# Two tiles' values and one tile's scores moved into the last chunk of the first layer of a two-layer fp32 kernel

## The chip, the core and the metric

The kernel runs on one core of a Trainium2 chip, in one launch, all of it in 32-bit floats. The core has five instruction queues that run side by side and wait for each other through semaphores: PE (TensorE, with its weight loads shown as PEld), DVE (VectorE), ACT (ScalarE), POOL (GpSimd) and SP (SyncE, which here only issues DMAs). The metric is the device time of one execution in microseconds (us), lower is better. Three runs of the kernel before took 5859.45, 5865.35 and 5869.25 us; the median is 5865.35 us.

## The reference, cut to what matters

The input `x` has 4 images of 384 channels by 64 by 64 pixels. Each of two layers normalises its input over groups of channels (`_gn`) and adds its result to that input.

```python
x = x + _L0_conv_ref(_gn(x), ...)   # a selective state-space layer over the 4096 pixels of an image
x = x + _L1_conv_ref(_gn(x), ...)   # an outlook-attention layer
```

The first layer projects each pixel to 768 channels and their gates, runs a causal convolution of 4 taps, derives a step size, `B` and `C` from it, and runs the recurrence `h = dA * h + dBx` over the 4096 pixels with 16 states a channel; the output is gated and projected back to 384 channels.

The second layer works on 3 by 3 windows at stride 2, 32 by 32 windows an image. For each window it needs scores and values:

```python
a = einsum('bchw,ac->bhwa', pooled, attn_w) + attn_b      # pooled: 2x2 means; 12 heads x 9 x 9 scores
a = softmax(a.reshape(B, L, HEADS, 9, 9) * scale)          # over the last axis
v = einsum('blkc,koc->blko', patches, conv_w)              # 9 pixels q of a window, a 384x384 matrix for each
o = einsum('bnlpq,bnlqd->bnlpd', a, v)                     # attention inside the window
out[..., ki::2, kj::2] += o                                # the windows are folded back with their overlaps
y = einsum('bchw,oc->bhwo', out, proj_w) + proj_b
```

## The kernel before, in words

**First layer** (`mamba_layer`). The 4 images are cut into 68 chunks of 241 pixels, 17 an image. The work of a chunk is 12 units of 64 channels, so 816 units; the main loop counts them as steps `s`, and chunk 67, the last, is steps 804 to 815. In step `s` the loop issues, for every engine, the parts of several units: DVE runs the two scans of unit `s` (`s_scan`, 128x968 each) and half of the products that feed unit `s+1` (`s_inputs2`); ACT makes the decays of unit `s+1` (`s_decay`, 8 exponentials into the two PSUM tiles `da0`, `da1`); POOL multiplies the states of unit `s-1` by `C` (`s_outputs`, 128x1928) and makes the other half of the products of unit `s+2` (`s_inputs`); PE sums the states of two units (`s_sum`) in every odd step. SP fetches `dxr` for units `s+4, s+5` and `dtr` for units `s+2, s+3` in every even step (`s_fetch`, `s_fetch_dt`). Each engine runs its instructions strictly in the order in which the Python code issues them: the helper `InOrder` fixes that, so an instruction that waits holds up all that its engine has behind it. Tile, the framework, puts in the semaphore waits. Its DMAs take eight semaphores in turn, whichever engine issues them: a DMA waits until the one eight places before it has landed.

The parts for the chunk to come (`plan`) end with the last chunk. `e_project`, `e_mean` and `e_store` (`ends`) project a finished chunk back, add up its statistics and store it to `x1` in DRAM; for chunk 67 they stand in steps 818 to 823, followed by the group norm of the last image (`group_norm_coeffs`: matmul `pm`, two ACT operations, matmuls `pv`, one DVE and one POOL operation, and the factors `sc1`, `bi1`, `bi4`).

**Second layer** (`outlook_layer`). An image is cut into 8 tiles of 8 pixel rows, 128 windows each, so 32 tiles. For each tile: three loads of its rows `xr`, pooled pixels `t2`, scores (six matmuls `psa<-wa,t2` of 128x486), a softmax (`at`, `mx`, `rs` on DVE, ACT and POOL), a store of the weights to DRAM (`ads`) and reads back as `ain` in another layout, block diagonals `bd` (ACT and POOL), 36 small matmuls `ps<-bd,vin` for each of four window rows (`p_attend`), six DVE adds into `fold` (`p_fold`), and the output projection (`pso`). The values of a tile are 9 products `psv<-wv,xp` (three matmuls of 128x384 each), copied by ACT and stored to DRAM, from where they come back as `vin`.

Tiles 0 to 21 have their values computed during the first layer, on pixels that are already normalised (class `Early`, functions `v_load` to `v_next`, up to chunk 65); they are marked by `c.vd`, and layer 2 only reads them. Their pooled pixels come from POOL (`pool_rows`) and the last product of the softmax is POOL's. Tiles 22 to 31 have no `vd`: their pixels are put in order by six ACT operations (`pixels`), and the nine products of tile `i+1` run on PE while tile `i` is attended (`p_values`). Tile 31 of the loop ends the kernel.

**Between the layers** (`outlook_before`). This is a generator that the main loop resumes once a step, at the end of the step, from `front_end`, step 803, on: the front of layer 1 is over then and its SBUF (right side) is free.

```python
        if s >= front_end:
            over = das[0] if s >= NU * len(chunks) - 1 else None
            behind(lambda: pmm.tile([P, 2, TM], F32, tag="mm", name="psv").rearrange("p a b -> p (a b)"), over)
```

Before the change it loads the rows of tile 0, writes zeros to the ends of some DRAM buffers, loads the value matrices `wv` (9 parts of 576 KB) in the steps 803 to 807, two a step, has POOL pool tile 0, loads `wa`, `ab`, `wpr`, `pb` and `own`, waits for step 815, and then has PE compute the scores of tile 0 into `da0`, which is free after the last scan. Four steps later it issues their softmax.

Of the kernel before, what the change touches and what calls it, by code (L numbers as in the profile page):

```python
# [7 lines left out]
F32 = mybir.dt.float32  # L8
AF = mybir.ActivationFunctionType
# [3 lines left out]
P = 128  # L13
C = 384
# [96 lines left out]
def mamba_layer(ctx, tc, x, w, x1, sc1, bi1, bi4, consts, early, behind):  # L111
# [837 lines left out]
    for s in range(-4, NU * (len(chunks) + 2)):  # L949
        k, m = divmod(s, NU)  # L950
        if m % 2 == 0 and unit(s + 4) is not None:
            s_fetch(s + 4)
        if m % 2 == 0 and unit(s + 2) is not None:
            s_fetch_dt(s + 2)
        parts(s, EARLY)
        if m % 4 == 3 or s >= NU * len(chunks):
            norm_part(False)

        if (u := unit(s + 1)) is not None:
            s_inputs2(u)  # L960
        if (u := unit(s - 3)) is not None and not u.first and u.j % 2:
            s_gate(u)
        parts(s, READY)

        b, ci = chunks[k][:2] if 0 <= k < len(chunks) else (B, 0)
        if b + 1 < B:
            n, e = divmod(NU * ci + m - 3, NU // 2)
            if e == 0 and 0 < n <= NCB * NX:
                x_stat(b + 1, n - 1, pending.pop())
            if e == 1 and 0 <= n < NCB * NX:  # L970
                pending.append(x_load(b + 1, n))
            if e == 2 and n == NCB * NX:
# [24 lines left out]
        if s >= front_end:  # L997
            over = das[0] if s >= NU * len(chunks) - 1 else None
            behind(lambda: pmm.tile([P, 2, TM], F32, tag="mm", name="psv").rearrange("p a b -> p (a b)"), over)


class OutlookTile:
# [146 lines left out]
def outlook_layer(ctx, tc, x1, w, out, sc1, bi1, bi4, weights, ready, tiles):  # L1149
# [23 lines left out]
        InOrder(tc, e) for e in (nc.tensor, nc.vector, nc.scalar, nc.gpsimd, nc.sync)  # L1173
    )

    wa, ab, wv, wpr, pb, own, vds, ads = (
        weights[name] for name in ("wa", "ab", "wv", "wpr", "pb", "own", "vds", "ads")
    )
    io = ctx.enter_context(tc.tile_pool(name="io1", bufs=3))
    act = ctx.enter_context(tc.tile_pool(name="act1", bufs=2))  # L1180
    pa = ctx.enter_context(tc.tile_pool(name="pa", bufs=1, space=bass.MemoryType.PSUM))
    pv = ctx.enter_context(tc.tile_pool(name="pv", bufs=3, space=bass.MemoryType.PSUM))
    pt = ctx.enter_context(tc.tile_pool(name="pt", bufs=1, space=bass.MemoryType.PSUM))

    def p_load(c):
        if c.vd is not None and c.i % 3 == 0 and tiles[c.i + 3].vd is not None:
            xr = act.tile([P, 3, NCB, ROWS, NW], F32, tag="xp", name="xr")
            xr = xr.rearrange("p k cb r w -> p (k cb r w)")[:, : NCB * ROWS * W]
            c.load(sp, x1, xr.rearrange("p (cb r w) -> p cb r w", cb=NCB, w=W))
            return  # L1190
        c.load(sp, x1, io.tile([P, NCB, ROWS, W], F32, tag="xr", name="xr", bufs=4))

    def p_pixels(c):
        t2 = act.tile([P, NCB, NR * NW], F32, tag="t2", name="t2")
        if c.vd is not None:
            t3 = act.tile([P, VQ, C], F32, tag="vst", name="t3", bufs=3).rearrange("p q c -> p (q c)")
            t3 = t3[:, : NCB * NR * W].rearrange("p (cb i j) -> p cb i j", cb=NCB, j=W)
            c.pool_rows(gp, ae, t2, t3, sc1, bi4)
            return
        t3 = act.tile([P, NCB, NR * NW], F32, tag="t3", name="t3", bufs=1)  # L1200
        xp = act.tile([P, 3, NCB, ROWS, NW], F32, tag="xp", name="xp")
        for _ in c.pixels(gp, ae, xp, sc1, bi1):
            pass
        c.pool(ve, t2, t3)
# [20 lines left out]
            )  # L1225

    def fetch(c, r, name, width, src):
        dst = act.tile([GW * KK, NGW, width], F32, tag=name, name=name, bufs=3)
        n = GW * KK
        row = r * NW * KK  # L1230
        full = min(NGW, (src.shape[0] - row) // n)
        sp.dma_start(dst[:, :full, :], src[row : row + full * n, :].rearrange("(g p) a -> p g a", p=n))
        if full < NGW:
            sp.dma_start(dst[: src.shape[0] - row - full * n, full, :], src[row + full * n :, :])
        return dst
# [7 lines left out]
    def p_blocks(c, r, part, parts):  # L1243

        n = GW * KK
        if part == 0:
            c.bd[r] = act.tile([n, NGW, GW, HO], F32, tag="bd", name="bd")
        bd = c.bd[r]
        mine = 1 + r % 2
        if part == 0:  # L1250
# [23 lines left out]
                    )  # L1274

    def p_clear(c):
        c.fold = fold = act.tile([P, NCB, ROWS, W + 2], F32, tag="fold", name="fold")
        if c.first:
            gp.memset(fold, 0.0)
        else:  # L1280
            gp.memset(fold[:, :, 1:, :], 0.0)
            gp.tensor_copy(fold[:, :, 0, :], tiles[c.i - 1].fold[:, :, ROWS - 1, :])
# [74 lines left out]
    for i in range(-1, len(tiles)):  # L1357
        mid, old = tile_at(i + 1), tile_at(i)
        even = mid is not None and (mid in ready or mid.vd is not None)
        for r in range(NR):  # L1360
            t = NR * i + r
            if i < 0 and r == 3:
                p_fetch_values(mid, 0)
            if old and r == 0 and i > 0:
                p_fetch_values(old, 0)
# [18 lines left out]
            if t == 1:  # L1384
                for c in ready:
                    p_load(c)
            c, k = ahead(old, mid, r + 1)
            qs = ((0, 1, 2), (3, 4), (5, 6), (7, 8))[r]
            for n, q in enumerate(qs):
# [31 lines left out]
                    stores.pop(0)()  # L1421


def outlook_before(ctx, tc, w, x1, H, W, sc1, bi4, dram, weights, ready, tiles):

    nc = tc.nc
    pe, ve, ae, gp, sp = (
        InOrder(tc, e) for e in (nc.tensor, nc.vector, nc.scalar, nc.gpsimd, nc.sync)  # L1430
    )
    NW = W // 2
    HO = HEADS * KK
    wp = ctx.enter_context(tc.tile_pool(name="wv1", bufs=1, side="right"))
    wv = weights["wv"] = wp.tile([P, NCB, KK, C], F32, tag="wv", name="wv")
    t2 = wp.tile([P, NCB, NR * NW], F32, tag="t2", name="t2")
    c = tiles[0]
    ready.append(c)
    with tc.tile_pool(name="before", bufs=1, side="right") as early:
        c.load(sp, x1, early.tile([P, NCB, ROWS, W], F32, tag="xr", name="xr"))  # L1440

        zero = early.tile([KK, C], F32, tag="zero", name="zero")
        gp.memset(zero, 0.0)
        vds = weights["vds"] = [dram.tile([P * KK + KK, C], F32, tag=f"vd{i}", name=f"vd{i}") for i in range(2)]
        ads = weights["ads"] = [dram.tile([P * KK + KK, HO], F32, tag=f"ad{i}", name=f"ad{i}") for i in range(3)]
        for v in vds:
            sp.dma_start(v[P * KK :, :], zero)
        for v in ads:
            sp.dma_start(v[P * KK :, :], zero[:, :HO])
        for q in range(KK):  # L1450
            sp.dma_start(wv[:, :, q, :], w["wv"][:, :, q, :])
            if q % 2:
                psum, over = yield
        c.pool_rows(gp, ae, t2, early.tile([P, NCB, NR, W], F32, tag="t3", name="t3"), sc1, bi4)
        yield
    wp = ctx.enter_context(tc.tile_pool(name="wp1", bufs=1, side="right"))
    na = HO * KK
    shapes = {
        "wa": [P, NCB, na],
        "ab": [P, na],  # L1460
        "wpr": [P, NCB, NCB, P],
        "pb": [P, NCB],
        "own": [GW * KK, GW],
    }
    for name, shape in shapes.items():
        weights[name] = wp.tile(shape, F32, tag=name, name=name)
    for cb in range(NCB):
        sp.dma_start(weights["wa"][:, cb], w["wa"][:, cb])
    for name in ("ab", "wpr", "pb", "own"):
        sp.dma_start(weights[name], w[name])  # L1470
    while True:
        psum, over = yield
        if over is not None:
            break
    parts = c.weights(
        pe, ve, ae, sp, over.rearrange("p (h a) -> p h a", h=2), wp, weights["wa"], weights["ab"], ads[0]
    )
    next(parts)

    for _ in range(4):  # L1480
        yield
    next(parts)
    next(parts, None)


@with_exitstack
def layers(ctx, tc, w, out):
# [24 lines left out]
    later = outlook_before(ctx, tc, w, x1, H, W, sc1, bi4, dram, weights, ready, tiles)  # L1512

    def behind(*room):
        try:
# [76 lines left out]
```

## Time and profile before

| what | us |
|---|---|
| median of three runs | 5865.35 |
| the profiled execution, its own time | 5861.92 |
| its span, first to last instruction | 5860.1 |
| PE, DVE, ACT, POOL busy | 5295.0, 5241.6, 4848.9, 5392.2 |
| first layer: last POOL product of the states ends at | 4955.4 |
| second layer: first attention matmul at | 4982.4 |

Every number below is in microseconds from the start of the span. In the views of the timeline a line is: start, duration, engine, source line (53 is the helper that records all operations), operation, output<-inputs, shapes, how many were merged, and in brackets the idle time of that engine before it with what ended it. The trace shows each 32-bit matmul of the program as two rows, so 27 matmuls of the program are 54 in it. "SPq" are DMA issues on SP. The line "PEclk" or the column of that name is the clock that TensorE was granted, as a part of full speed.

### The profile page before, as it was taken

Reading aid. Unit: us, or ns where it says so; the run is one execution under the profiler, and the core shown is the slowest. Engines: PE = TensorE matmul, PEld = TensorE weight load, DVE = VectorE, ACT = ScalarE, POOL = GpSimd, SP = SyncE. Lnnn points to the kernel's source line nnn. Section 1 sums busy time; section 2 is a strip of 40 time slices with the busy share of each in tenths; the row PEclk is TensorE's granted clock in tenths of the full one; section 3 lists DMA queues with packets and bytes.
Section 4 is the critical chain, followed back from the end, with each engine's and each line's share of the span. In section 5 each row is a group of like instructions: output and inputs, shape, how many; then the busy total and the mean of one; then the engine's idle time right before and its main releaser. Section 6 shows DMA issues by size and latency. Waiting matters only on the chain.

```text
span 5860.1 us, 126156 instructions
## 1 busy us (share of the span) xinstructions
PE 5295.0 (90%) x46114; PEld 3820.7 (65%) x46114; DVE 5241.6 (89%) x4269; ACT 4848.9 (83%) x13283; POOL 5392.2 (92%) x2045
## 2 busy tenths in 40 slices
PE   6888888888999999998999999999999995899999
PEld 5666666666666666666666666666666663666555
DVE  4999999999999999999999999999999997787444
ACT  4888888888888888888898888889889885677665
POOL 3999999999999999999999999999999998899433
PEclk9999999999999999999999999999999997999999
DMA  4555554445666666666666666656666655666444
GB/s 133 145 142 143 143 144 134 131 131 139 166 169 174 171 179 162 173 171 159 176 177 174 179 168 171 170 148 173 170 167 169 162 152 158 199 211 206 159 168 154
DMA packets 758875, 955.11 MB, mean 163 GB/s; under 512 B 211488, under 2 KB 660972, under 8 KB 758124
## 3 DMA queue, kind: packets, MB, share of 16 engines
q1 hardware_dynamic: 758252, 947.04, 58.7%
q8 instruction: 362, 5.93, 0.4%
q14 instruction: 261, 2.14, 0.1%
HBM read 720.92 MB, written 225.70 MB: 162 GB/s over the span
## 4 chain that ended last, share of the span: by engine, by line
ACT 36%; PE 25%; DVE 17%; DMA 5%; POOL 5%; SPq 4%; issue 4%; DVEq 0%; ACTq 0%; POOLq 0%
ACT da L53 20%; DVE h L53 14%; PE ps_in L53 4%; SPq L53 4%; POOL h L53 4%; PE ps_v L53 4%; PE y L53 3%; PE psv L53 3%; ACT L53 3%; PE ps_cv L53 2%; PE ps L53 2%; ACT zs L53 2%; PE pso L53 2%; ACT xc L53 2%; PE psa L53 2%
## 5 line engine op out<-in xcount | busy, mean ns | idle before, releaser
L53 DVE TENSOR_TENSOR_SCAN h<-da,h 128x968 f32<-128x968 f32 x1632 | 3453.9, 2158 | 151.6 <-POOL h L53 74.7
L53 POOL TENSOR_TENSOR h<-h,bc 128x1928 f32<-128x1928 f32 x816 | 3231.1, 3960 | 45.2 <-DVE h L53 41.3
L53 ACT ACTIVATE da<-dtr,alog 128x241 f32<-128x241 f32 x6528 | 2657.5, 455 | 370.0 <-DVE h L53 291.1
L53 POOL TENSOR_TENSOR h<-dxr,bc 128x964 f32<-128x964 f32 x816 | 1622.8, 1989 | 65.7 <-DMA dxr<-dxd 48.7
L53 PE MATMUL ps_in<-u,win 128*128 128x241 f32 x4824 | 1056.9, 370 | 37.2 <-ACT xb L53 26.4
L53 PEld LDWEIGHTS ps_in<-u,win 128*128 128x128 f32 x4824 | 903.7, 190 | 161.2 <-ACT xb L53 49.1
L53 DVE TENSOR_TENSOR h<-dxr,bp 128x964 f32<-128x964 f32 x816 | 928.7, 1138 | 10.5 <-DMA dxr<-dxd 9.2
L53 PE MATMUL y<-h,ssum 128*32 128x241 f32 x13056 | 782.9, 373 | 70.9 <-POOL h L53 70.7
L53 PE MATMUL ps_cv<-xb,cdiag 128*128 128x241 f32 x3264 | 718.1, 373 | 26.6 <-ACT zs L53 21.3
L53 PEld LDWEIGHTS ps_cv<-xb,cdiag 128*128 128x128 f32 x3264 | 606.3, 190 | 133.7 <-issue 34.0
L53 PEld LDWEIGHTS y<-h,ssum 128*32 128x32 f32 x13056 | 434.6, 111 | 343.6 <-POOL h L53 93.3
L53 POOL TENSOR_TENSOR bd<-ain,own 99x1188 f32<-99x1188 f32 x192 | 431.0, 2266 | 211.4 <-PE ps L53 196.9
L53 PE MATMUL ps_out<-zs,wout 128*128 128x241 f32 (+1 forms) x2448 | 563.8, 382 | 0.0
L53 ACT ACTIVATE bd<-ain,own 99x216 f32<-99x216 f32 (+1 forms) x1408 | 467.5, 420 | 113.1 <-PE ps L53 102.2
L53 PEld LDWEIGHTS ps_out<-zs,wout 128*128 128x128 f32 x2448 | 489.2, 200 | 43.2
L53 PE MATMUL ps_v<-wq,xo 128*32 128x384 f32 x4752 | 425.0, 489 | 32.4 <-ACT xr L53 29.8
L53 DVE TENSOR_TENSOR fold<-fold,ps 128x192 f32<-128x192 f32 (+1 forms) x768 | 210.3, 302 | 185.2 <-PE ps L53 171.8
L53 PE MATMUL ps_dt<-xd,wdt 128*128 128x241 f32 x816 | 227.1, 403 | 91.4 <-ACT xd L53 52.9
L53 PEld LDWEIGHTS ps_v<-wq,xo 128*32 128x32 f32 x4752 | 140.8, 110 | 240.5 <-issue 163.3
L53 PE MATMUL pso<-fold,wpr 128*128 128x256 f32 (+6 forms) x990 | 275.4, 425 | 3.7 <-DVE fold L53 3.3
L53 PE MATMUL ps<-bd,vin 99*32 99x99 f32 (+1 forms) x9216 | 228.2, 250 | 46.4 <-DVE fold L53 21.1
L53 PEld LDWEIGHTS ps<-bd,vin 99*32 99x32 f32 (+1 forms) x9216 | 200.5, 109 | 102.8 <-issue 44.8
(128 smaller groups left out, 5544.8 us busy)
## 6 DMA issues: line engine op xcount, KB each, us to landing
dxr<-dxd SPq DMA_DIRECT2D x1632, 120.5 KB
dtr<-dtd SPq DMA_DIRECT2D x1632, 120.5 KB
wq<-in_wv SPq DMA_DIRECT2D x297, 192.0 KB
dxd<-dtx SPq DMA_DIRECT2D x816, 60.2 KB
dtd<-dt SPq DMA_DIRECT2D x272, 180.8 KB
ve<-v SPq DMA_DIRECT2D x198, 192.0 KB
bc<-bcd SPq DMA_DIRECT2D x272, 120.5 KB
vin<-ve SPq DMA_DIRECT2D x66, 445.5 KB
```

Source lines behind the costliest of these rows:

```text
L53: made = self.tc.keep_in_program_order(issue(*args, **kwargs))
```

## The change

The generator is rewritten, `outlook_layer` gets its buffers from other pools, and tiles 22 and 23 get a `vd`.

1. Nothing but allocations stands in step 803. In step 804 come the zeros, the rows of tile 0 and a third of `wa`, in step 805 the rest of `wa`; `wv` is loaded by ninths, part `q` in step 805+q; `ab` and `own` in step 814. `wpr` and `pb` are loaded by layer 2 itself, in its second step of tile 0.
2. POOL pools tile 0 in step 806. The scores of tile 0 are computed in three parts of 128x324 in steps 807 to 809, each copied from PSUM by ACT (`ae.mul`); the softmax is issued in step 815, not 819.
3. Tile 22: rows loaded in step 807, put in order in step 808 (`put`), its nine values computed in steps 809 to 815: one a step, two in steps 812 and 814. Each is copied by ACT, which also issues its store (`ae.dma_start`).
4. Tile 23: rows loaded in step 815, put in order in step 816, its nine values in step 825, one after the other. On PE they come between the matmul `pm` and the matmuls `pv` of the last group norm.
5. `outlook_layer`: `ain`, `vin`, `bd`, `fold` come from a pool `hot`, `xp` and `t3` from `far`, `wpr` and `pb` from `wp1`; the numbers of buffers are unchanged. The first `vin` is fetched as the first DMA of the layer, not behind the first `ain` and `xr`. In the loop over tiles only tiles 24 to 31 compute their values.

```diff
-            over = das[0] if s >= NU * len(chunks) - 1 else None
-            behind(lambda: pmm.tile([P, 2, TM], F32, tag="mm", name="psv").rearrange("p a b -> p (a b)"), over)
+            behind(lambda: pmm.tile([P, 2, TM], F32, tag="mm", name="psv"), s >= NU * len(chunks) - 1)
...
+    hot = ctx.enter_context(tc.tile_pool(name="hot1", bufs=2))
+    far = ctx.enter_context(tc.tile_pool(name="far1", bufs=2))
+    wp = ctx.enter_context(tc.tile_pool(name="wp1", bufs=1))
+    wpr = wp.tile([P, NCB, NCB, P], F32, tag="wpr", name="wpr")
+    pb = wp.tile([P, NCB], F32, tag="pb", name="pb")
...
-        if c.vd is not None and c.i % 3 == 0 and tiles[c.i + 3].vd is not None:
-            xr = act.tile([P, 3, NCB, ROWS, NW], F32, tag="xp", name="xr")
+        if c.vd is not None and c.i % 3 == 0 and tiles[c.i + 2].vd is not None:
+            xr = far.tile([P, 3, NCB, ROWS, NW], F32, tag="xp", name="xr")
...
-            if i < 0 and r == 3:
+            if i < 0 and r == 0:
                 p_fetch_values(mid, 0)
...
                 for c in ready:
                     p_load(c)
+                sp.dma_start(wpr, w["wpr"])
+                sp.dma_start(pb, w["pb"])
...
+        def values(i, q):
+            v = staged()
+            psv = room().rearrange("p a b -> p (a b)")[:, :C]
+            last[i].values(pe, wv, q, psv)
+            ae.copy(v, psv)
+            ae.dma_start(last[i].vd.rearrange("(p q) c -> p q c", q=KK)[:, q, :], v)
+
+        def scores(h):
+            psa = room().rearrange("p a b -> p (a b)")[:, :NH]
+            for cb in range(NCB):
+                pe.matmul(
+                    psa, t2[:, cb, :], wa[:, cb, h * NH : (h + 1) * NH], start=(cb == 0), stop=(cb == NCB - 1)
+                )
+            ae.mul(at[:, h * NH : (h + 1) * NH], psa, 0.25)
...
+            for q in {1: (0,), 2: (1,), 3: (2,), 4: (3,), 5: (4,), 6: (5,), 7: (6,), 8: (7,), 9: (8,)}.get(n, ()):
+                load_wv(q)
+            if 3 <= n < 6:
+                scores(n - 3)
+            if n == 3:
+                last[0].load(sp, x1, rows())
...
+        GROUP = {4: (("put", 0),), 5: ((0, 0),), 6: ((0, 1),), 7: ((0, 2),), 8: ((0, 3), (0, 4)), 9: ((0, 5),), 10: ((0, 6), (0, 7)), 11: ((0, 8), ("load", 1)), 12: (("put", 1),), 13: (), 14: (), 15: (), 16: (), 21: ((1, 0), (1, 1), (1, 2), (1, 3),(1, 4), (1, 5), (1, 6),(1, 7), (1, 8)), 22: ()}
+
+        for n in range(max(GROUP) + 1):
+            room, over = yield
+            first(n)
+            for item in GROUP.get(n, ()):
+                if item[0] == "put":
+                    put(item[1])
+                elif item[0] == "load":
+                    last[item[1]].load(sp, x1, rows())
+                else:
+                    values(*item)
+            if over and not done:
+                done.append(n)
+                softmax()
...
+    last = tiles[len(early.tiles) : 3 * NT]
+    for i, c in enumerate(last):
+        c.vd = dram.tile([P * KK, C], F32, tag=f"vl{i}", name=f"vl{i}")
```

The `n` of the diff is the step less 804.

More of the change, by code (lines that the diff above doesn't have):

```diff
@@ L1174, in outlook_layer @@
     )
-    wa, ab, wv, wpr, pb, own, vds, ads = (
-        weights[name] for name in ("wa", "ab", "wv", "wpr", "pb", "own", "vds", "ads")
-    )
+    wa, ab, wv, own, vds, ads = (weights[name] for name in ("wa", "ab", "wv", "own", "vds", "ads"))
     io = ctx.enter_context(tc.tile_pool(name="io1", bufs=3))
     act = ctx.enter_context(tc.tile_pool(name="act1", bufs=2))
+    hot = ctx.enter_context(tc.tile_pool(name="hot1", bufs=2))
[3 more added lines that the diff above has]
+    pb = wp.tile([P, NCB], F32, tag="pb", name="pb")
     pa = ctx.enter_context(tc.tile_pool(name="pa", bufs=1, space=bass.MemoryType.PSUM))
@@ L1199, in p_pixels @@
             return
-        t3 = act.tile([P, NCB, NR * NW], F32, tag="t3", name="t3", bufs=1)
-        xp = act.tile([P, 3, NCB, ROWS, NW], F32, tag="xp", name="xp")
+        t3 = far.tile([P, NCB, NR * NW], F32, tag="t3", name="t3", bufs=1)
+        xp = far.tile([P, 3, NCB, ROWS, NW], F32, tag="xp", name="xp")
         for _ in c.pixels(gp, ae, xp, sc1, bi1):
@@ L1227, in fetch @@
     def fetch(c, r, name, width, src):
-        dst = act.tile([GW * KK, NGW, width], F32, tag=name, name=name, bufs=3)
+        dst = hot.tile([GW * KK, NGW, width], F32, tag=name, name=name, bufs=3)
         n = GW * KK
@@ L1246, in p_blocks @@
         if part == 0:
-            c.bd[r] = act.tile([n, NGW, GW, HO], F32, tag="bd", name="bd")
+            c.bd[r] = hot.tile([n, NGW, GW, HO], F32, tag="bd", name="bd")
         bd = c.bd[r]
@@ L1276, in p_clear @@
     def p_clear(c):
-        c.fold = fold = act.tile([P, NCB, ROWS, W + 2], F32, tag="fold", name="fold")
+        c.fold = fold = hot.tile([P, NCB, ROWS, W + 2], F32, tag="fold", name="fold")
         if c.first:
@@ L1421, in outlook_layer, with outlook_before @@
                     stores.pop(0)()
-def outlook_before(ctx, tc, w, x1, H, W, sc1, bi4, dram, weights, ready, tiles):
+def outlook_before(ctx, tc, w, x1, H, W, sc1, bi1, bi4, dram, weights, ready, tiles, last):
     nc = tc.nc
@@ L1433, in outlook_before @@
     HO = HEADS * KK
+    na = HO * KK
+    NH = na // 3
     wp = ctx.enter_context(tc.tile_pool(name="wv1", bufs=1, side="right"))
-    wv = weights["wv"] = wp.tile([P, NCB, KK, C], F32, tag="wv", name="wv")
-    t2 = wp.tile([P, NCB, NR * NW], F32, tag="t2", name="t2")
+    shapes = {"wv": [P, NCB, KK, C], "wa": [P, NCB, na], "ab": [P, na], "own": [GW * KK, GW]}
+    for name, shape in shapes.items():
+        weights[name] = wp.tile(shape, F32, tag=name, name=name)
+    wv, wa, ab = (weights[name] for name in ("wv", "wa", "ab"))
@@ L1437, in outlook_before @@
     c = tiles[0]
     ready.append(c)
+    vds = weights["vds"] = [dram.tile([P * KK + KK, C], F32, tag=f"vd{i}", name=f"vd{i}") for i in range(2)]
+    ads = weights["ads"] = [dram.tile([P * KK + KK, HO], F32, tag=f"ad{i}", name=f"ad{i}") for i in range(3)]
     with tc.tile_pool(name="before", bufs=1, side="right") as early:
-        c.load(sp, x1, early.tile([P, NCB, ROWS, W], F32, tag="xr", name="xr"))
-        zero = early.tile([KK, C], F32, tag="zero", name="zero")
-        gp.memset(zero, 0.0)
@@ L1444, in outlook_before @@
[L1444 to L1450, printed above, removed]
-            sp.dma_start(wv[:, :, q, :], w["wv"][:, :, q, :])
-            if q % 2:
-                psum, over = yield
@@ L1454, in outlook_before @@
[L1454 to L1483, printed above, removed]
+        pixels = lambda: early.tile([P, 3, NCB, ROWS, NW], F32, tag="xp", name="xp")
@@ new lines, in outlook_before, with load_wv @@
+        rows = lambda: early.tile([P, NCB, ROWS, W], F32, tag="xr", name="xr")
+        staged = lambda: early.tile([P, C], F32, tag="v", name="v1", bufs=3)
+        at = early.tile([P, na], F32, tag="at", name="at")
+        mx = early.tile([P, HO], F32, tag="mx", name="mx")
+        rs = early.tile([P, HO], F32, tag="rs", name="rs1")
+        t2 = early.tile([P, NCB, NR * NW], F32, tag="t2", name="t2")
+        def load_wv(q):
+            sp.dma_start(wv[:, :, q, :], w["wv"][:, :, q, :])
+        def values(i, q):
[4 more added lines that the diff above has]
+            ae.dma_start(last[i].vd.rearrange("(p q) c -> p q c", q=KK)[:, q, :], v)
@@ new lines, in scores, with put, first @@
+        def scores(h):
[5 more added lines that the diff above has]
+            ae.mul(at[:, h * NH : (h + 1) * NH], psa, 0.25)
+        def put(i):
+            for _ in last[i].pixels(gp, ae, pixels(), sc1, bi1):
+                pass
+        def first(n):
+            if n == 0:
+                zero = staged()[:KK]
+                gp.memset(zero, 0.0)
+                c.load(sp, x1, rows())
+                sp.dma_start(wa[:, 0], w["wa"][:, 0])
+                for v in vds:
+                    sp.dma_start(v[P * KK :, :], zero)
+                for v in ads:
+                    sp.dma_start(v[P * KK :, :], zero[:, :HO])
+            if n == 1:
+                sp.dma_start(wa[:, 1], w["wa"][:, 1])
+                sp.dma_start(wa[:, 2], w["wa"][:, 2])
+            if n == 2:
+                t3 = pixels().rearrange("p k cb r w -> p (k cb r w)")[:, : NCB * NR * W]
+                c.pool_rows(gp, ae, t2, t3.rearrange("p (cb i j) -> p cb i j", cb=NCB, j=W), sc1, bi4)
+            for q in {1: (0,), 2: (1,), 3: (2,), 4: (3,), 5: (4,), 6: (5,), 7: (6,), 8: (7,), 9: (8,)}.get(n, ()):
[4 more added lines that the diff above has]
+                last[0].load(sp, x1, rows())
+            if n == 10:
+                sp.dma_start(ab, w["ab"])
+                sp.dma_start(weights["own"], w["own"])
@@ new lines, in softmax @@
+        def softmax():
+            qs = at.rearrange("p (q a) -> p q a", q=KK)
+            ve.tensor_add(at, at, ab)
+            ve.reduce_max(mx, at.rearrange("p (q a) -> p a q", q=KK), AX.X)
+            ve.tensor_sub(qs, qs, mx.unsqueeze(1).to_broadcast([P, KK, HO]))
+            ae.activation(at, at, AF.Exp, scale=float(HD) ** -0.5)
+            ve.reduce_sum(rs, at.rearrange("p (q a) -> p a q", q=KK), AX.X)
+            ve.reciprocal(rs, rs)
+            ve.tensor_mul(qs, qs, rs.unsqueeze(1).to_broadcast([P, KK, HO]))
+            sp.dma_start(ads[0][: P * KK, :].rearrange("(p q) a -> p (q a)", q=KK), at)
@@ new lines, in outlook_before @@
+        done = []
+        GROUP = {4: (("put", 0),), 5: ((0, 0),), 6: ((0, 1),), 7: ((0, 2),), 8: ((0, 3), (0, 4)), 9: ((0, 5),), 10: ((0, 6), (0, 7)), 11: ((0, 8), ("load", 1)), 12: (("put", 1),), 13: (), 14: (), 15: (), 16: (), 21: ((1, 0), (1, 1), (1, 2), (1, 3),(1, 4), (1, 5), (1, 6),(1, 7), (1, 8)), 22: ()}
[12 more added lines that the diff above has]
+                softmax()
@@ L1511, in layers @@
         c.vd = dram.tile([P * KK, C], F32, tag=f"ve{i}", name=f"ve{i}")
-    later = outlook_before(ctx, tc, w, x1, H, W, sc1, bi4, dram, weights, ready, tiles)
+    last = tiles[len(early.tiles) : 3 * NT]
+    for i, c in enumerate(last):
+        c.vd = dram.tile([P * KK, C], F32, tag=f"vl{i}", name=f"vl{i}")
+    later = outlook_before(ctx, tc, w, x1, H, W, sc1, bi1, bi4, dram, weights, ready, tiles, last)
     def behind(*room):
```

## The prediction

> **What bounds the kernel now.** I read first the busy time by windows, which says what binds each stage; its columns are window, length, busy us of PE, PEld, DVE, ACT and POOL with counts, then granted TensorE clock, busy share of the DMA engines, GB/s.
>
> ```profile
> 4900.00:4950.00 50.00, 22.99 (x178) 12.06 (x178) 46.99 (x29) 35.99 (x106) 49.71 (x18) 0.67 0.58 168
> 5200.00:5250.00 50.00, 46.88 (x758) 33.68 (x757) 42.56 (x86) 35.55 (x102) 48.23 (x27) 1.00 0.68 211
> 5600.00:5650.00 50.00, 50.00 (x436) 28.87 (x428) 24.74 (x46) 31.45 (x83) 19.32 (x12) 1.00 0.53 175
> ```
>
> The last chunk of layer 1 (4900) is POOL's: 49.71 of 50, with PE half idle and 14 us of ACT free. Tiles with stored values (5200) are POOL's, with PE close behind. Tiles that compute values (5600) are PE's: 50.00 of 50, POOL under half busy. So two tiles' values stand where they cost full price, and there is PE time free in the last chunk.
>
> Then the timeline of POOL: the clearing of `fold` marks each tile's start (here tiles 0, 1, 2, 4, 20, 21, 22 and 31).
>
> ```profile
> 4981.67 1.59 POOL L53 MEMSET fold<- 128x1782 f32 x1
> 5014.82 1.42 POOL L53 MEMSET fold<- 128x1584 f32 x1
> 5042.42 1.42 POOL L53 MEMSET fold<- 128x1584 f32 x1
> ...
> 5083.83 1.42 POOL L53 MEMSET fold<- 128x1584 f32 x1
> ...
> 5424.92 1.42 POOL L53 MEMSET fold<- 128x1584 f32 x1
> 5442.08 1.42 POOL L53 MEMSET fold<- 128x1584 f32 x1
> 5482.10 1.42 POOL L53 MEMSET fold<- 128x1584 f32 x1
> ...
> 5821.45 1.42 POOL L53 MEMSET fold<- 128x1584 f32 x1
> ```
>
> Tiles 4 to 20 take (5424.92 - 5083.83) / 16 = 21.3 us each, tiles 22 to 31 (5821.45 - 5482.10) / 9 = 37.7. The first two are slow, 33.2 and 27.6: the layer starts with empty buffers.
>
> Third, the timeline of the last chunk, for what a burst of loads does to the scans, and of the change of layers, for its chain.
>
> ```profile
> 4883.33 5.58 DMA wv<-in_wv
> 4888.93 5.08 DMA dtr<-dtd
> ```
>
> ```profile
> 4894.12 1.63 ACT L53 ACTIVATE da<-dtr,alog 128x241 f32<-128x241 f32 x4 [10.41 <-DMA dtr<-dtd]
> ...
> 4900.22 3.92 POOL L53 TENSOR_TENSOR h<-h,bc 128x1928 f32<-128x1928 f32 x1 [2.17 <-DVE h L53]
> ```
>
> ```profile
> 4969.97 0.38 PE L53 MATMUL pm<-mv,blk 128*128 128x1 f32 x2 [2.33 <-DVE mv L53]
> ...
> 4972.18 0.30 ACT L53 ACTIVATE bi<-neg,sc 128x1 f32<-128x1 f32 x1 [1.29 <-POOL sc L53]
> ...
> 4973.33 1.29 SPq L53 DMA_DIRECT2D xr<-x  x3
> ```
>
> Two parts of `wv` (the first fence, from the chain of waits) went ahead of `dtr`; ACT stood 10.41 us, but POOL lost only 2.17, since DVE's scans ran some 5 us ahead of it (scan of unit 805 ended at 4887.1, POOL took it at 4892.2). At the end, in the same timeline, PE does the scores of tile 0 (`da<-wa`, 5.68 at 4951.02), the last projection (`ps_out`, to 4967.6), then `pm`; `bi` follows at once, and behind `bi` tile 1's rows are fetched.
>
> **The change, part by part.** Sums are against the profiled execution, 5861.92 (span 5860.1 and 1.8 around it); the median of the runs is 3.43 higher.
>
> *Two tiles fewer with values in layer 2.* Two periods of 37.7 become 21.3: -32.8. Bounds: at most the PE work of 18 products, -35 (a product is 1.94: ACT's copies of two successive ones end-on-end start at 5456.53 and 5458.47); at least 2 x (37.4 - 22.3) = -30, by the shortest late and longest early period there is. The change of kind costs no more than now: tile 20 takes 17.2 (its successors need no pooling by POOL) and tile 21 takes 40.0; the two move to tiles 22 and 23.
>
> *The values of tile 22 in the last chunk.* PE: 9 x 1.94 = 17.5 at full clock, 35 at the 0.50 that idle windows show; it has 27 free of 50. ACT, until the last decays: 8 copies of 0.48, six `xp` operations of 4.18 together, three copies of scores of about 0.45 (nearest: 0.48 for 384 columns), 8 DMA issues. An issue on ACT is not in the trace; bounds are 0 and SP's longest usual 0.6, I take SP's 0.34 for a store of values. Sum 12.1, against 14 free in 50 us: hidden, thinly. Does ACT's wait for PE close a loop? A copy waits for its product, that one in odd steps for the state sum, which waits for POOL's product of two units earlier; behind the copy are the next decays, the scan, POOL again. Once round: POOL 3.96 + sum 3.43 + product at half clock 3.9 + copy and issue 0.8 + decay 1.63 + two scans 4.3 = 18 us for four units, which take POOL 4 x 5.83 = 23.3. So POOL stays the bound: 0, at worst the 8 us that 12.1 less some 4 us of lead would expose. The Trainium skill's page "TensorE: Matmul & The Clock Gate", section "Part 1: The HAM clock gate", says the array runs at half clock until it has been busy some 3.4 us and again after as long an idle window; the 0.50 agrees. By it alone tile 23's products (below) would lose some 1.7 us (an estimate from that page) if PE cooled before them, and the sum would be -18.5 and not -20.2; the gap ahead of them is 2.8 us by my sum, so I take them at full clock.
>
> *`wv` by ninths, one a step, and the zeros a step later.* `dtr` for units 806, 807 now goes out ahead of all loads, so the 2.17 us of POOL's wait go. What is late next: `dtr` of 808, behind `wa` and the first ninth (about 1.6 MB behind POOL's clearing of the zeros, near 4886), which at the 283 GB/s of the saturated stretch 4884 to 4928 land at about 4896; it is needed at about 4898. Then `dtr` of 810, behind two ninths and tile 22's rows (2.0 MB, 7 us): in time by about nothing. POOL's own work is the same but for one 0.15 clearing. Term: -2; bounds -2 and +8 (the same cover as above, both cannot use it).
>
> *The scores' move.* PE's 5.68 before the last state sum go, but the gate of the last two units is now behind the softmax on DVE: after the last scan 1.16 + 1.94 + 1.17, exponential 1.01 on ACT behind the copy of the ninth value, 1.96 + 0.83 + 1.17. That ends at about 4958, as the gate's own input does; gate near 4958.8 (before 4958.95). Of the seven matmuls of the first `ps_out` only the last two need the gate, and PE has the other five done by then, so the three `ps_out` (2.85 each) end at about 4965.3 and not 4967.6; `pm` at 4967.7. With the term above, -2.3 here in all.
>
> *The values of tile 23.* Nine products of 1.94 = 17.5 us stand on PE between `pm` and `pv`, with nothing else for PE to do: `pv` moves from 4970.2 to about 4985.5. Behind it wait DVE and POOL (the group norm), ACT's `bi`, then its block diagonals, POOL's, and SP: the fetch of tile 1's rows waits for `bi` and goes from 4973.33 to about 4987.6, with every `ain`, `vin` and `xr` behind it. Its landing (5.7 us before), POOL's pooling and ACT's scaling lead to tile 1's scores, which began at 4985.40, 3 us late behind tile 0's first attention; they now begin at about 4997. That is +11.6, and all that follows hangs on it (softmax of tile 1, its weights). Bounds: +4, if the 18 us by which tiles 0 and 1 exceed 2 x 21.3 take up waits; +19, if the whole 17.5 and a cold clock come through.
>
> *`wpr` and `pb` in layer 2*: 576 KB in a stretch where the DMA share is 0.96 to 1.04, 2.1 us of transfer; between 0 and 2.1 I take 1. *The first `vin` ahead*, *other pools* (same number of buffers): 0, off the chain; a rival below.
>
> Sum: -32.8 - 0 + 11.6 (with the -2.3 in it) + 1 = -20.2. 5861.92 - 20.2 = 5841.7; on the median 5865.35 - 20.2 = 5845.
>
> **The rivals.**
>
> *The start of layer 2 absorbs the delay.* `vin` is there early, tile 0's rows and matrices have long landed, and POOL (2.8, 1.9) and PE (11) waits for DMA stand in the trace there. Then the change of layers costs some 4: -32.8 + 4 = -29, 5836. Against it: tile 1's chain is serial and starts with a fetch that is late by 14.
>
> *The change of layers or the last chunk costs more.* +19 in place of +11.6, or half of the 8 us above: -9 to -13, 5852 to 5857.
>
> *Slower: bursts of loads ahead of `dtr`.* Place: steps 804 to 814. If every burst is exposed for its transfer plus 2.5 us, as `dtr` was for the 10.41: tile 0's rows, `wa` and a ninth 2.95 MB, 13 us; two ninths with rows 2.0 MB, 10; two pairs of ninths with stores 1.4 MB each, 7.5 each; 38, less 5 of lead, 33; with the -2 gone, -32.8 + 33 + 13.6 + 1 = +15, 5880. It turns slower when 20 us of POOL time are lost. For it: 10.41 us seen for 1.2 MB. Against: only 2.17 reached POOL, and each ninth now has a step of 5.83 us for itself.
>
> *The other pools slow the tiles.* 24 tiles of 21.3 at 22.2 would undo the gain. Nothing in the profile speaks for it.
>
> **How the numbers follow.** Forecast (5839 to 5851) 0.5; start absorbs 0.2; costs more 0.2; slower by bursts 0.06; by pools or anything else 0.04. Leaving out the last two and the far ends gives 5831 to 5859. 0.2% is 11.7 us, about what a measurement of this kernel tells from no change: faster than 5853.6 is the forecast, the absorbing start and half of the costlier case, 0.80; within 0.2% the other half and a little of the slower ones, 0.13; slower 0.07.
>
> **What would show it.** After: `fold` of tile 0 cleared near 4995, of tile 1 near 5026, tile 23's nine products as 54 rows in a row ending near 4985, eight tiles of 37.7 and no more, the last `fold` cleared near 5801, no wait of ACT for `dtr` above 3 us, POOL's last product of states near 4953. It is wrong if POOL idles by more than 5 us in 4885 to 4955, if tiles 4 to 20 leave 21.3, or if tile 1 starts outside 5019 to 5034.

## The result, and the profile after

The changed kernel takes 5850.54 us (median of 18 runs, 5847.55 to 5859.18) against 5861.82 for the kernel before on the same chip (18 runs, 5857.36 to 5869.85): a ratio of 0.9983, 95% interval 0.9977 to 0.9989; the medians are 11.3 us apart. That is just inside the 0.2% that the prediction took as the least difference a measurement tells from no change. The forecast was 5845 with a range of 5831 to 5859: the sign is right, and of the 20.2 us a little over half is there.

The profiled execution took 5859.18, which is the longest of the 18; its span is 5857.4. So single profiles are compared below by distances inside them, mostly from the end of POOL's last product of states (4955.41 before, 4955.70 after), and times by the ratios of many runs.

The busy time by windows of the changed kernel, for the three stretches shown of the kernel before (columns as there):

```profile
4900.00:4950.00 50.00, 42.94 (x266) 24.78 (x260) 43.55 (x27) 38.93 (x107) 49.92 (x20) 0.88 0.82 243
5200.00:5250.00 50.00, 47.34 (x833) 35.30 (x832) 42.25 (x81) 34.58 (x99) 47.53 (x27) 1.00 0.66 206
5600.00:5650.00 50.00, 50.00 (x466) 28.77 (x468) 27.29 (x44) 27.77 (x72) 14.80 (x10) 1.00 0.58 190
```

PE is now 42.94 of 50 busy in the last chunk, and POOL still has no gap (49.92): tile 22's values fit in. The timeline of POOL, tiles 1, 4, 20, 21, 22, 23, 24 by the clearing of `fold`:

```profile
5038.34 1.42 POOL L53 MEMSET fold<- 128x1584 f32 x1
...
5108.32 1.41 POOL L53 MEMSET fold<- 128x1584 f32 x1
...
5450.30 1.43 POOL L53 MEMSET fold<- 128x1584 f32 x1
5471.68 1.41 POOL L53 MEMSET fold<- 128x1584 f32 x1
5492.41 1.43 POOL L53 MEMSET fold<- 128x1584 f32 x1
5511.59 1.42 POOL L53 MEMSET fold<- 128x1584 f32 x1
5549.97 1.59 POOL L53 MEMSET fold<- 128x1782 f32 x1
```

Tiles 4 to 20 take (5450.30 - 5108.32) / 16 = 21.4 each, as before, and tiles 21 and 22 now take 20.7 and 19.2 (40.0 and 37.4 before). But tile 1 starts at 5038.34, 23.5 later than before. The timeline of the change of layers (POOL, DVE, PE and SP together) shows where that comes from:

```profile
4943.98 11.72 POOL L53 TENSOR_TENSOR h<-h,bc 128x1928 f32<-128x1928 f32 x3
...
4949.50 7.22 DVE L53 TENSOR_TENSOR at<-at,ab 128x972 f32<-128x972 f32 x1
...
4964.93 0.65 DVE L53 TENSOR_TENSOR zs<-y,zs 128x482 f32<-128x482 f32 x1
4965.64 1.97 PE L53 MATMUL ps_out<-zs,wout 128*128 128x241 f32 x4 [5.83 <-DVE zs L53]
...
4977.51 0.38 PE L53 MATMUL pm<-mv,blk 128*128 128x1 f32 x2 [2.33 <-DVE mv L53]
...
4996.94 0.28 PE L53 MATMUL pv<-mv,blk 128*128 128x1 f32 x2
...
4998.62 1.29 SPq L53 DMA_DIRECT2D xr<-x  x3
```

The softmax's first addition, which the prediction took at 1.16, is 7.22 long: it starts behind the last scan and ends at 4956.72, 1.02 behind POOL's three products. The last gate (`zs<-y,zs`) stands behind the softmax on DVE and comes 9.23 behind POOL's end, not 3.54 as before; `pm` comes 21.81 behind and not 14.56. Then PE does tile 23's products, 19.43 from `pm` to `pv`, before the fetch of tile 1's rows can go.

By stages, in us, the forecast's terms put into the same distances:

| stage | before | forecast | after |
|---|---|---|---|
| POOL, from its product `h<-dxr` for unit 801 (issued in step 799) to its last product of states | 100.47 | 98.5 | 98.45 |
| POOL's last product to tile 1 | 59.41 | 72.6 | 82.64 |
| tile 1 to tile 31 | 806.63 | 774.8 | 776.23 |
| tile 31 to the end of the span | 38.65 | 38.65 | 42.83 |

One line is off by 10 and one by 4; the others came as forecast. The prediction had named a start of tile 1 outside 5019 to 5034 as a sign that it is wrong, and tile 1 started at 5038.34.

### The profile page after: what moved, and what is told of

Same layout as the page of the kernel before. It is cut to its first block, busy times and chain, and to the rows that moved or that the text cites. A ratio compares the mean times of both kernels' runs of the same rounds, so it can differ in the third digit from the quotient of the medians.

```text
span 5857.4 us, 126295 instructions
## 1 busy us (share of the span) xinstructions
PE 5302.0 (91%) x46156; PEld 3835.2 (65%) x46156; DVE 5248.9 (90%) x4267; ACT 4834.5 (83%) x13288; POOL 5405.2 (92%) x2051
## 3 DMA queue, kind: packets, MB, share of 16 engines
q10 hardware_dynamic: 2592, 3.54, 0.2%
```

## The experiments

Theory A: DVE's operations with two operands in SBUF get nothing done while POOL's products run back to back, so the softmax, put ahead of the last gate, waits for POOL and takes the gate with it; tile 23's values cost, besides, about what the prediction said. Rivals: the addition is slow for another reason (its operand `ab` lands late), the start of layer 2 absorbs what is gained, or tile 23's values are worth more or less than thought. The marks of all profiles, behind POOL's last product, and the ratios of time to the kernel before on the same chip (one profile a row: two of the same kernel differ by up to 4 us at tile 31):

| kernel | gate | `pm` | tile 1 | tile 31 | ratio |
|---|---|---|---|---|---|
| before | 3.54 | 14.56 | 59.41 | 866.04 | 1 |
| changed | 9.23 | 21.81 | 82.64 | 858.87 | 0.9983 (0.9977 to 0.9989) |
| changed, again | 9.23 | 21.94 | 82.31 | 854.87 | 0.9981 (0.9972 to 0.9989) |
| softmax late | 1.92 | 12.95 | 72.37 | 848.71 | 0.9973 (0.9964 to 0.9983) |
| softmax late, again | 1.93 | 12.97 | 72.68 | 849.98 | 0.9968 (0.9955 to 0.9980) |
| no addition | 6.05 | 15.87 | 74.33 | 850.58 | one run |
| only tile 22 | 9.22 | 21.47 | 66.65 | 868.10 | 0.9993 (0.9984 to 1.0002) |
| values behind `bi` | 9.26 | 20.75 | 79.09 | 857.68 | 0.9983 (0.9974 to 0.9992) |
| late, behind `bi` | 2.38 | 14.58 | 71.82 | 852.15 | 0.9967 (0.9955 to 0.9980) |
| late, only tile 22 | 1.92 | 12.95 | 58.02 | 859.02 | 0.9984 (0.9975 to 0.9993) |
| late, neither tile | 3.46 | 14.49 | 59.63 | 866.84 | 0.9992 (0.9983 to 1.0000) |
| late, only tile 22, `far` | 1.93 | 12.96 | 57.08 | 851.37 | 0.9973 (0.9962 to 0.9984) |
| late, tile 23 in tile 0 | 1.92 | 12.96 | 83.81 | 868.38 | 0.9999 (0.9990 to 1.0008) |
| the same, stores on ACT | 1.93 | 12.96 | 74.98 | 854.78 | 0.9980 (0.9971 to 0.9989) |

**The softmax behind the last gate.**

```diff
-            if over and not done:
-                done.append(n)
+            if n == 14:
                 softmax()
```

> One edit to the changed kernel: tile 0's softmax is issued three steps later, behind the last gate, as in the kernel before; its scores stay where the change put them. Theory A (VectorE's addition of two SBUF operands makes no progress while POOL's last three state products run): the addition takes 1.2 us instead of 7.22, the last gate comes 2 to 3 us behind POOL's last product (9.2 in the changed kernel), pm is 7 to 9 us earlier against POOL's last product, and the time falls by 7 to 10 us, to about 5842. Rival B (the addition is slow by its own shapes or because its operand ab lands late): it takes about 7 us here too, now behind the gate, pm waits for the end of the softmax, and the gain is under 3 us. Rival C (the start of layer 2 absorbs what the gate gains): the addition is short and pm early, but tile 1's start moves by less than 3 us.

The timeline of this kernel at the change of layers:

```profile
4942.15 11.75 POOL L53 TENSOR_TENSOR h<-h,bc 128x1928 f32<-128x1928 f32 x3
...
4955.82 0.66 DVE L53 TENSOR_TENSOR zs<-y,zs 128x482 f32<-128x482 f32 x1 [8.06 <-PE y L53]
4956.40 1.16 DVE L53 TENSOR_TENSOR at<-at,ab 128x972 f32<-128x972 f32 x1
...
4966.85 0.38 PE L53 MATMUL pm<-mv,blk 128*128 128x1 f32 x2 [2.32 <-DVE mv L53]
4967.10 17.66 PE L53 MATMUL psv<-wv,xp 128*128 128x384 f32 x54
4984.59 0.28 PE L53 MATMUL pv<-mv,blk 128*128 128x1 f32 x2
```

The same addition takes 1.16 once POOL is done; the gate waits only for PE's state sum, `pm` is 8.9 earlier against POOL's end, and tile 1 starts 10.3 earlier. Rivals B and C are out. The time falls from 0.9983 to 0.9973; the intervals overlap, so both kernels were run a second time. The run again, beside the last kernel of this section:

> The late softmax alone, again, to be compared on one chip with the next kernel. Theory A: 0.997 of the kernel before; tile 1 starts 72 to 73 us behind POOL's last product, the last tile 848 to 850 behind it.

It has the same marks within 1.3. The two runs of the changed kernel have a mean ratio of 0.9982, the two of this one 0.9970: some 7 us, about what the marks of tile 31 differ by in the mean (856.9 against 849.3).

**The addition left out.** This kernel computes tile 0's softmax without its bias.

```diff
-            ve.tensor_add(at, at, ab)
             ve.reduce_max(mx, at.rearrange("p (q a) -> p a q", q=KK), AX.X)
```

> One edit to the changed kernel: the addition of the attention's bias for tile 0 alone is left out; the rest of the softmax stays where the change put it. Theory A: the maximum, with one operand in SBUF, runs beside POOL in its usual 1.96 us; the subtraction, which is next and has two SBUF operands, now meets POOL's product and takes about 5 us instead of 1.17, ending about 1 us behind POOL's last product; the gate comes about 6 us behind POOL's last product instead of 9.2, so some 3 us are gained. Rival B (late ab): the softmax runs through in 8 us from the last scan, all 6 to 7 us come back and the gate waits for the state sum, 2 to 3 us behind POOL. A third way, that the maximum is held as well, would show as a maximum of over 4 us.

Its timeline:

```profile
4940.22 11.76 POOL L53 TENSOR_TENSOR h<-h,bc 128x1928 f32<-128x1928 f32 x3
...
4945.75 1.94 DVE L53 TENSOR_REDUCE mx<-at 128x108 f32<-128x972 f32 x1
...
4947.73 5.28 DVE L53 TENSOR_TENSOR at<-at,mx 128x972 f32<-128x972 f32 x1
...
4958.03 0.65 DVE L53 TENSOR_TENSOR zs<-y,zs 128x482 f32<-128x482 f32 x1
```

The maximum runs beside POOL in its usual time, and the hold moves on to the next operation with two SBUF operands: 5.28, ending 1.03 behind POOL. The gate comes at 6.05, as expected. With `ab` out of the program, a late `ab` can't be the reason. This settles theory A for the gate.

**Tile 23 left to layer 2.**

```diff
-    last = tiles[len(early.tiles) : 3 * NT]
+    last = tiles[len(early.tiles) : 3 * NT - 1]
...
-        GROUP = {... 11: ((0, 8), ("load", 1)), 12: (("put", 1),), ... 21: ((1, 0), ... (1, 8)), 22: ()}
+        GROUP = {... 11: ((0, 8),), 12: (), ... 22: ()}
```

> One part of the change undone: tile 23's rows, pixels and values are left to layer 2 as before; tile 22's stay in the last chunk. Theory A (the nine products stand on the path for their 19.4 us and more): pv follows pm at once, tile 1's fetch of rows goes 19 us earlier against pm, tile 1's scores 19 to 23 us earlier, and tile 23 takes 37.7 instead of 21.3, so the time falls by 3 to 7 us against the changed kernel, to 5844 to 5848. The prediction's sum (13.9 for the values against 16.4 saved) expects it 2.5 us slower than the changed kernel, 5853. If layer 2's start absorbs most of the delay, it is 8 us or more slower, 5858.

My theory's number was wrong: tile 1 started 16.0 earlier and not 19 to 23, and the time was not lower than that of the changed kernel but some 6 us higher (0.9993 against 0.9983). Tile 23 took its 15 more again, but tile 18 took 28.5 instead of 21.1 as well (from its clearing to the next, as tiles are counted above; an expectation below calls it tile 19). What that was is told below.

**Tile 23's products behind `pv` and `bi`.**

```diff
-        GROUP = {... 21: ((1, 0), (1, 1), ... (1, 8)), 22: ()}
+        GROUP = {... 23: ((1, 0), (1, 1), ... (1, 8))}
```

> One edit to the changed kernel: tile 23's nine products are issued two steps later, behind pv and bi, ahead of tile 0's attention. Tile 1's fetch of rows then goes about 17 us earlier against pm, while TensorE's and ACT's order keeps tile 0's attention behind the nine copies. Theory A (what delays layer 2 is TensorE's and ACT's queue): tile 1's scores gain only 2 to 4 us, and the time falls by 3 to 6 us. Rival (the prediction's: the delay is that of the chain pv, bi, fetch): tile 1's scores gain 10 us or more and so does the time.

The fetch of tile 1's rows goes 2.7 behind `pm` instead of 21.1, and tile 1 starts 3.5 earlier, no more (1.1 of them because `pm` itself came earlier): behind the nine copies on ACT stand tile 0's block diagonals, and its attention stands behind the nine products on PE. So the queues, and not the fetch alone, carry the delay. In the time no gain is seen (0.9983).

**The changed kernel again, and three combinations on one chip.**

> The changed kernel itself, beside the three that follow, so that they can be compared on one chip. Theory A: 0.998 of the kernel before. In its trace VectorE's addition takes about 7 us again, tile 1's fold is cleared 82 to 83 us behind POOL's last state product (59.4 in the kernel before), and the last tile's about 859 behind it.

> Two edits together: tile 0's softmax behind the last gate and tile 23's products behind pv and bi. Theory A (both act on the same stretch, one after the other): tile 1 starts 68 to 70 us behind POOL's last product (72.4 with the softmax alone, 79.1 with the products alone), so the time is 3 to 4 us below that of the late softmax alone and some 13 below the changed kernel, 0.996 of the kernel before. Rival (with pm early there is nothing left for the second edit, since TensorE's queue sets the start): 72, as with the first edit alone.

> Late softmax, and tile 23's values left to layer 2: what remains is tile 22. Theory A: tile 1 starts 57 to 58 us behind POOL's last product, 15 less than with tile 23's values there; tile 23 costs its 15 to 16 in layer 2 again; the time is within 3 us of that of the late softmax with both tiles: tile 23 is worth nothing where it was put. If tile 23's values are worth moving, this kernel is 5 us or more slower than the late softmax with both tiles; if they cost more than they save, 5 or more faster.

> Late softmax, and the values of both tiles left to layer 2: of the change remain wv by ninths, the early scores, the first vin ahead, the pools and the two loads in layer 2. Theory A: tile 1 starts 57 to 58 us behind POOL's last product, the last chunk is some 2 us shorter than in the kernel before, and the time is 2 to 5 us below it, 0.9993; against the kernel with tile 22 alone it is 15 to 17 us slower, the full price of a tile's values, since those of tile 22 are hidden in the last chunk. If they are not hidden, the difference is under 12 and POOL's last product comes later with them, against the first step of the chunk.

The edits are those above, put together; in the third, `GROUP` is empty, no tile is in `last`, and the load of tile 22's rows in step 807 is gone. The changed kernel repeats its marks (82.3; the addition 6.43, ending at 4956.99, 1.03 behind POOL again). The second edit adds nothing to the late softmax (71.82 against 72.37): here the rival was right. With neither tile, tile 1 starts at 59.6, as in the kernel before and not at 57 to 58, and the first stage of the table above is 98.27: the 2 us there come from the new order of the loads, which this kernel keeps, and tile 22's values cost the stage 0.2 (98.43 to 98.51 in every kernel that has them). My expectation that tile 22 alone gains 15 to 17 us on this failed at first sight, 7.8 by tile 31, and so did the one that tile 22 alone is within 3 us of both tiles: it came 10 later at tile 31. Again tile 18 had taken 28.6 in the kernel with tile 22 alone.

**What held tile 18.** In both kernels with tile 22 alone SP stands at one DMA. The timeline of SP in "late, only tile 22":

```profile
5373.12 0.36 SPq L53 DMA_DIRECT2D out<-ot  x1
5381.31 1.29 SPq L53 DMA_DIRECT2D xr<-x  x3
5382.71 0.32 SPq L53 DMA_DIRECT2D ain<-ad  x1
5383.13 0.81 SPq L53 DMA_DIRECT2D vin<-ve  x2
```

The rows of tile 21 wait 7.8 for a row buffer, with `ain` and `vin` behind them. In the changed kernel these rows go into a buffer of the pool `far`, which the condition in `p_load` grants if the tile two further on has its values; with tile 23 late it has not. So the edit that undid tile 23 had brought a wait of its own. With that mended:

```diff
-        if c.vd is not None and c.i % 3 == 0 and tiles[c.i + 2].vd is not None:
+        if c.vd is not None and c.i % 3 == 0 and tiles[c.i + 1].vd is not None:
```

> Late softmax, tile 22 alone, as before, but tile 21's rows go into the buffers of the far pool as those of tiles 18 and 15 do. In both kernels with tile 22 alone tile 19 took 28.5 us instead of 21.1, and in their traces SyncE stands about 8 us at tile 21's rows, waiting for one of the four row buffers, with a vin and the stores behind it. Theory A (this wait belongs to that edit and not to tile 23): tile 19 takes 21 to 22, tile 1 starts 57 to 59 us behind POOL's last product, the last tile 850 to 853 (848.7 for the late softmax with both tiles), so the time is 0.9973 to 0.9977 of the kernel before: tile 23's move is worth 2 to 4 us. Rival: tile 19 keeps its 28 us, and tile 23's move is worth about 10.

Tile 18 takes 21.55, and tile 31 comes at 851.37, against 848.71 and 849.98 with both tiles: tile 23's move is worth some 2 us, not to be told from nothing in the time (0.9973 against 0.9970). And tile 22's is worth 866.84 - 851.37 = 15.5 by these marks, of which 2.5 lie ahead of tile 1; the times (0.9992 and 0.9973, each with some 0.001 to either side) say about 11.

**Tile 23's values inside layer 2.** PE has idle time in tile 0, so the products were tried there, with their rows loaded ahead of tile 1's (`late` is tile 23; `extra` is called at the end of each step):

```diff
+        if (i, r) == (-1, 0):
+            late.load(sp, x1, io.tile([P, NCB, ROWS, W], F32, tag="xr", name="xr", bufs=4))
+        if (i, r) == (0, 0):
+            for _ in late.pixels(gp, ae, far.tile(...), sc1, bi1): pass
+        for q in {(0, 0): (0, 1, 2), (0, 1): (3, 4), (0, 2): (5, 6), (0, 3): (7, 8)}.get((i, r), ()):
+            ...
+            late.values(pe, wv, q, psv[:, :C])
+            ae.copy(late.vst[:, q % VQ, :], psv[:, :C])
+            if q % VQ == VQ - 1:
+                sp.dma_start(late.vd...[:, q - VQ + 1 : q + 1, :], late.vst)
```

> Late softmax, tile 22 in the last chunk, and tile 23's rows, pixels and nine products spread over the four steps of tile 0 in layer 2, behind each step's attention, their stores on SyncE. The products leave the path of pm, pv, fetch; TensorE is busy only 12 of 20 and 13 of 21 us there. Theory A (tile 23 cost 13 us only for where it stood): tile 1 starts 58 to 63 us behind POOL's last product, what is lost in tiles 0 to 3 is under 8 us, and the time is 5 to 10 us below that of the late softmax alone, 0.9956 to 0.9964. Rival (the start of layer 2 is bound by its transfers, and 2.7 MB more cost about what the products did): tiles 0 to 3 take 10 us or more longer, and the time is that of the late softmax alone.

It lost all: tile 1 started at 83.8, over 20 us later than theory A has it, and the time is that of the kernel before. SP's timeline in this kernel:

```profile
4969.19 1.75 SPq L53 DMA_DIRECT2D xr<-x  x3
4997.88 0.32 SPq L53 DMA_DIRECT2D vl<-vst  x1
4998.25 0.39 SPq L53 DMA_DIRECT2D vin<-ve  x1
4998.74 0.68 SPq L53 DMA_DIRECT2D ain<-ad  x1
```

SP stands 27 us ahead of the first store, waiting for ACT's copy, with a `vin` and an `ain` of the next steps behind it. So the stores were given to ACT, whose copies they follow anyway (`ae.dma_start`, the pixels in step (-1, 3), three products in each of the steps (0, 1) to (0, 3)):

> As the kernel with tile 23's products in tile 0, but their stores are issued on ACT, and the pixels one step earlier and the products one step later (three in each of the last three steps of tile 0). Theory: that kernel lost its gain where SyncE waited 27 us at the first store for ACT's copy, with vin, ain and xr of the next steps behind it; without that wait tile 1 starts 60 to 70 us behind POOL's last product and the last tile 840 to 847, so the time is 2 to 9 us below the late softmax alone. Rival (the transfers and the products themselves cost as much there): tile 1 starts 75 us or more behind, and the time is not below the late softmax alone.

Tile 1 comes 8.8 earlier than that (74.98), but the rival is right: it is no faster than the late softmax (0.9980 against 0.9968 on the same chip). In its trace POOL gets tile 1's rows, which land behind tile 23's, 26.6 behind its last product and not 23.0 as in the kernel with tile 22 alone, and in the chain of waits products of tile 23 (5.80 us) stand between the two halves of tile 2's scores. I found no place for tile 23 that is better than beside the norm. No kernel tried is clearly faster than the one with the softmax late, 0.997, some 17 us below the kernel before and 7 below the changed one.

## Why the prediction was half right

- *Two tiles fewer in layer 2, -32.8 and +1.* Tile 1 to tile 31 went from 806.63 to 776.23 (772.56 in the second profile): -30.4 and -34.1, as forecast. The change of kind moved on from tiles 20 and 21 (57.2 for the two) to 22 and 23 (57.6) without a price, and the other pools show none: tiles 4 to 20 take 21.4 for 21.3.
- *Values of tile 22 at 0.* Right: 0.2 in the last chunk. ACT waits for no `dtr` at all in the stretch, POOL for nothing. Nearly the whole saving of a tile comes from here, 15.5 by the marks and about 11 by the times.
- *`wv` by ninths at -2.* Right: 100.47 to 98.45. The rival of bursts ahead of `dtr` is out.
- *The scores' move.* This step failed: "after the last scan 1.16 + 1.94 + 1.17". It took 1.16 from this row of the kernel before:

```profile
4959.53 1.16 DVE L53 SCALAR_TENSOR_TENSOR at<-da,ab 128x972 f32<-128x972 f32 x1
```

There POOL did nothing, and one operand (`da0`) lay in PSUM; where the softmax was put, both operands lay in SBUF and POOL had three products of 3.9 to do. The forecast had the gate 5.4 behind POOL's end (4958.8 against 4953.4) and `pm` 14.3 behind; they came 9.23 and 21.81 behind. Of the 10.0 by which tile 1 missed the forecast, 3.8 are the gate; 3.7 lie from the gate to `pm` (12.6 for the 8.9 worked out; the kernel without the addition takes 9.8, so the working was 0.9 short, and the rest is PE's, which after a wait of 5.83 did 12 rows of the projection in 4.12 and not 2.61, at a granted clock of 0.50 up to 4971); 1.9 are tile 23's products, 19.4 for 17.5; and 0.6 is left over. By the kernel with the softmax late, the whole place of the softmax cost 10.3.
- *Values of tile 23, +11.6 with the 2.3 in it.* Right but for the hold. With the softmax late, tile 1 starts 72.4 behind POOL, where the forecast's 5026 and 4953.4 give 72.6; that they agree so closely is partly luck, since `pm` came 1.4 earlier than forecast there and the way from `pm` to tile 1 took 1.1 longer. Against the kernels with tile 22 alone (58.0 and 57.1) tile 23 costs 14 to 16 ahead of tile 1, where 13.9 was worked out, and it saves 17 to 18 between tile 1 and tile 31 (794.29 against 776.34 and 777.30). What is left at tile 31, 2.7 and 1.4, is about the two or three us that the sum gave it.
- *The rival "the change of layers costs more"* is what came, by 10.0 at tile 1 where it had 7.4 (+19 in place of +11.6), but through DVE and not through the norm or the fetch. The measured difference, 11.3, is that rival's 9 to 13. That the time itself, 5850.54, still lies inside the forecast's 5839 to 5851 is luck: the prediction started from three runs with a median of 5865.35, and 18 runs gave 5861.82. *The start absorbs* did not come.
- *The end, at 0.* The last tile took 38.65 before and 40.0 to 42.8 in all 13 profiles since. In the changed kernel's chain of waits this stands in it, and not in that of the kernel before:

```profile
5841.38 5.10 DMA vin<-vd
```

PE waited 1.12 for this last `vin`, which is a quarter of the 4.2. Another 1.4 are two groups of PE's rows there, 2.40 and 6.38 long and not 1.75 and 5.64, with the granted clock at 0.50 for longer, and 1.6 lie behind PE's last row. Which part of the change brings this was not tried.

The sum of the marks (-2.0, +23.2, -30.4, +4.2) is -5 in the first profile and -9 in the second; the median says -11. The profiled executions were on the long side, and what shortens the others I can't show.

The kernel before had shown the price of the addition. The groups of DVE by form, in its tiles with stored values (5060 to 5430, POOL 94% busy) and, in the second fence, in those that compute them (5500 to 5800, POOL 39% busy):

```profile
L53 DVE TENSOR_TENSOR at<-at,mx 128x972 f32<-128x972 f32 x17 | 45.6, 2684 | 0.0
...
L53 DVE SCALAR_TENSOR_TENSOR at<-psa,ab 128x972 f32<-128x972 f32 x17 | 19.7, 1159 | 0.0
```

```profile
L53 DVE TENSOR_TENSOR at<-at,mx 128x972 f32<-128x972 f32 x8 | 9.4, 1171 | 0.3
```

The same subtraction takes 2684 ns in the mean in the first stretch and 1171 in the second, while the addition with one operand in PSUM keeps 1159 beside the busy POOL. The Trainium skill says it on the page "GPSIMD Engine Reference", section "1. Specifications": POOL's SBUF interfaces are shared with VectorE and contend with its instructions that have two SBUF inputs. And the Trainium skill's page "Trainium Architecture — The Big Picture", section "What this means for kernel authors", calls it an exclusive lock and no split of bandwidth. The runs agree with both: 7.22, 6.43 and 5.28 for the held operations, all ending 1.02 to 1.03 behind POOL's last product, so that of 1.16 us of work some 0.1 was done before it, and POOL's three products between 11.72 and 11.79 with them or without.

## What to carry to other kernels

Price an operation by a row in which the other engines do what they will do beside it, not by its shortest row; a spread within one form (here means of 1.2 and 2.7 us) is a question to be asked before it is moved. The scans, products and gates that DVE runs beside POOL in the first layer have one operand in PSUM; the operation that had not was put ahead of the last gate. And work moved into idle time of one engine is worth what its old place cost less what waits behind it in the queues of the new one: by the marks, tile 22 brought 15.5 of 16.4 us, tile 23, the same work, about 2.

## What was not expected of the hardware

Three POOL products in a row leave DVE no gap at all: an operation of 1.16 us ready at 4949.50 ended behind the third, though the third began only at 4951.77. DVE's maximum (1.94) and its scans (8.36 for four), whose second operand is in PSUM, run beside the same products in their usual time.

The clock after a short gap is not the same from one execution to the next. PE's gap between the last projection and `pm` is 2.3 us in all of them (the prediction had 2.8). The windows of the next 5 us in the two profiles of the late softmax:

```profile
4967.00:4972.00 5.00, 5.00 (x17) 3.03 (x18) 0.00 (x0) 1.42 (x4) 0.00 (x0) 1.00 0.84 263
```

```profile
4969.00:4974.00 5.00, 4.98 (x12) 3.11 (x13) 0.00 (x0) 0.94 (x3) 0.00 (x0) 0.66 0.82 265
```

In the first the granted clock stays at 1.00 and tile 23's products take 17.66; in the second, the same program, it is 0.66 and they take 19.10. The changed kernel has 0.66 in the 5 us behind `pm` as well, in both profiles; there the products begin at full clock, and the drop comes within the first microsecond. The Trainium skill's page "TensorE: Matmul & The Clock Gate", section "Part 1: The HAM clock gate", has the array slow down after an idle window of some 3.4 us; the loss of about 1.7 that the prediction worked out from it was seen, but after a gap of 2.3, and not each time.
